# Two graph layers on 64 graphs, one core: the last two graphs' leaky ReLU, output and softmax sums on other engines, and new orders for the first and last four graphs

## The chip, the cores and the metric

The kernel runs on one core of a Trainium2 chip. TensorE (PE in the profile, PEld for its weight loads), VectorE (DVE), ScalarE (ACT), GpSimd (POOL) and SyncE (SP, which issues the DMAs) each work through their own queue in order and wait on semaphores for one another. The metric is the device time of one execution in microseconds.

## The reference

There are 64 graphs of 256 nodes with 256 features, and an adjacency of zeros and ones. Everything is float32. Each graph passes two layers, cut here to what matters:

```python
# layer 0: attention (8 heads of 32), values chosen by edge type, then a feed-forward of 1024
attn = softmax(q @ k.T / sqrt(32))
out = sum((attn * (adj == r)) @ v[r] for r in range(4))      # adj is 0 or 1
x = ln(src + out @ Wo); x = ln(x + gelu(x @ W1) @ W2)
# layer 1: attention over the edges only, with a leaky ReLU on the scores
e = q @ k.T; e = where(e >= 0, e, 0.2 * e)
h = softmax(where(adj > 0, e, -9e15)) @ v
y = ln(concat(ln(h), x) @ Wffn.T) * g2 + b2 + x
```

## The kernel before

One graph is a program of about 122 to 142 operations ("op" in the code), each with one engine, the tiles that it reads and writes, and the instructions that it emits. All programs are put into one list by `in_order`. A graph in the middle takes the due times of `STARTS`, moved by 50 per graph (`PERIOD`). The first four graphs take theirs from `FIRST`, the last four from `LAST`: one number for each op of that graph, of which only the order matters. Each engine's queue is that list, cut down to the engine. Graphs overlap: while one is in layer 1, the next one or two are in layer 0. Tiles come from pools with a few buffers each (`TAGS`), so an op may also wait for a buffer: the score tiles "s" have two, the general PSUM tiles "g" four.

An op is named here by graph and by the tile that it writes, with #2 or #3 for the second or third op on it: 63.e10/0#3 is the third on pair 0 of e10 in graph 63. Scores are kept transposed, keys on partitions, in two halves of 128 keys. A head group hg has four heads, in two pairs (tile names end in hg, a slash and the pair).

In layer 1, after q1 and k1 (ACT copies), each head group runs as follows. TensorE makes the scores s1{hg}0 and s1{hg}1 (`score`, L486). DVE adds the mask, `e = s + neg` (`without_edges`, L511). ACT makes `m = relu(4 s)` (L760). POOL adds `e + m` (L764): with the factor 0.2 in the exp that follows, this is the leaky ReLU. ACT takes the exp (L502). POOL adds the two key halves into es (`halves_added`, L555). TensorE multiplies e with v1 into po[:, 0] (L524) and sums es over the partitions, with ones, into po[:, 1] (L529; `weighted`). DVE divides (L538, L541; `divide`) and takes a minimum for the flags (L546). The heads are turned by TensorE in the edge graphs (L413, through DRAM in the others), normalised (statistics L453 to L457, rs on POOL L462), multiplied with wf (pwa, L365), combined with zb (L784), normalised again (L468), and POOL multiplies by the gain (y2#2, L478) and adds x2 (y2#3, L795) before SP writes the output (L799).

After the last graph DVE checks the flags of all graphs (L807 to L811), TensorE sums over partitions (L813) and DVE writes `bad` (L814). Every engine then loads `bad` and branches past the general path, which isn't needed with these inputs.

The loads of the head are issued by SP in the order of the list: graph 0's x, xT and adj, the weights one by one (`fetch`, L567), and graph 1's.

Of the kernel before, what the change touches and what calls it, by code (L numbers as in the profile page):

```python
# [45 lines left out]
def in_order(programs, starts, period, first, last):  # L46
# [4 lines left out]
    for g, p in enumerate(programs):  # L51
# [75 lines left out]
        -6994.431, -7388.927, -7351.284, -6940.069, -6630.912, -6492.737, -5820.245, -6499.204, -6211.612, -6887.475,  # L127
        -6574.591, -6055.325, -6943.269, -6592.592, -5632.691, -6966.961, -6679.901, -5916.261, -5878.661, -5841.069,
        -7096.532, -7512.778, -6608.876, -6221.265, -5453.387, -5549.194, -6903.347, -6536.598, -6869.405, -6714.282,
        -6284.532, -5847.047, -6310.727, -6096.209, -6434.914, -6237.614, -6127.158, -6105.417, -5766.143, -6278.346,  # L130
        -6188.116, -6047.072, -5658.535, -5527.11, -5365.693, -5365.113, -5411.001, -6000.275, -5717.717, -5900.816,
        -5831.595, -5599.592, -5869.516, -5660.321, -5366.528, -5646.017, -5207.025, -5020.63, -4993.703, -4567.281,
        -4816.977, -4750.625, -4591.773, -4460.957, -4413.934, -4100.038, -4091.573, -4307.485, -3363.907, -4090.816,
        -4014.886, -3947.886, -3817.945, -3833.07, -3724.476, -4057.127, -4027.222, -2952.664, -2920.602, -2866.671,
        -2847.171, -2739.652, -2737.672, -2691.114, -2690.49, -2653.828, -2574.6, -2574.5, -2571.161, -2538.838,
        -2515.46, -2508.392, -2484.851, -2490.055, -2485.753, -2475.11, -2272.412, -1985.028, -1658.536, -1821.102,
        -1771.211, -2129.859, -2036.177, -2076.279, -2024.103, -1654.946, -1088.24, -2129.857, -2050.296, -1834.238,
        -1668.747, -1615.521, -888.839, -844.65, -844.648, -683.087, -2000.703, -2000.701, -1941.643, -1634.963,
        -1305.159, -1117.717, -1867.441, -1519.838, -1476.409, -1286.636, -1065.545, -947.048, -921.545, -905.763,
        -905.336, -659.96, -595.355, -586.09, -600.581, -562.092, -520.989, -499.765, -423.732, -332.149, -138.121,  # L140
        -71.149,
    ],
    [
        -6349.705, -5836.753, -6081.533, -4963.07, -4074.802, -4413.528, -5758.476, -5490.569, -5746.337, -5168.607,
        -5091.359, -4429.3, -4497.965, -4455.15, -5110.005, -4958.379, -4959.155, -4405.675, -4700.068, -5095.014,
        -4918.509, -4648.701, -4492.326, -3784.815, -3591.688, -3574.676, -3462.153, -4751.298, -4193.609, -4058.489,
        -3830.368, -4078.272, -4312.267, -4230.291, -4098.36, -4165.072, -3469.86, -3405.792, -3346.63, -3256.756,
        -3129.133, -3092.291, -3028.461, -2890.16, -2860.984, -2786.263, -2765.467, -2709.294, -1973.087, -2700.693,
        -2592.979, -2679.762, -2547.379, -2572.287, -2562.658, -2234.13, -2091.658, -1352.855, -1285.594, -1154.839,
        -1080.771, -1050.188, -1025.134, -1025.132, -1013.455, -1012.874, -989.144, -989.142, -966.626, -966.624,  # L150
        -860.071, -906.663, -558.44, -710.078, -678.573, -659.959, -657.563, -356.96, -279.865, -204.83, -153.563,
        -570.142, -497.868, -564.88, -400.824, -310.575, -155.647, -529.609, -492.619, -440.991, -372.152, 81.224,
        207.883, 207.885, 208.698, 207.885, -485.015, -297.546, -326.274, -30.803, -30.801, 140.805, -207.171,
        -420.509, 88.779, 94.889, 201.19, 208.257, 208.915, 212.631, 209.017, 218.342, 218.376, 220.881, 220.872,
        226.278, 226.28, 226.608, 226.657, 279.353, 279.888, 293.911,
    ],
    [
        -3383.624, -3282.358, -3383.821, -3315.719, -3292.114, -3276.51, -3278.393, -3143.603, -3202.947, -3127.58,
        -2580.644, -2247.869, -2579.025, -2435.009, -2777.309, -2722.09, -2626.561, -2402.135, -2620.893, -2656.961,
        -2631.065, -2219.459, -2622.132, -2116.303, -2108.283, -1937.208, -2022.273, -2592.872, -2572.894, -2577.864,  # L160
        -2373.389, -2294.93, -2442.259, -2482.641, -2247.275, -2242.874, -2220.102, -2131.046, -2130.146, -2134.458,
        -1791.22, -1730.871, -1604.611, -1586.638, -1465.435, -1440.682, -1117.654, -1046.213, -1042.05, -1130.19,
        -786.309, -989.513, -966.393, -1038.083, -990.527, -1025.728, -1009.818, -865.964, -811.776, -127.986,
        -65.354, 9.746, 82.436, 89.841, 104.183, 109.011, 131.966, 147.965, 147.967, 147.969, 147.971, 147.973,
        166.758, 166.76, 167.18, 214.884, 258.715, 170.464, 170.466, 170.298, 171.246, 185.358, 190.852, 208.774,
        208.776, 175.642, 180.624, 178.747, 185.531, 195.315, 196.259, 178.105, 180.761, 186.235, 190.215, 200.258,
        210.901, 213.291, 215.22, 214.541, 183.413, 187.736, 194.296, 194.298, 196.561, 205.853, 191.477, 188.038,
        192.651, 199.259, 201.622, 209.186, 211.426, 212.75, 212.71, 215.222, 217.141, 221.416, 221.418, 221.42,
        222.631, 226.586, 226.588, 226.78, 228.592, 259.663, 263.707, 276.031,
    ],  # L170
    [
        -2288.419, -2839.379, -2739.277, -1968.859, -600.823, -607.784, -1652.07, -1598.871, -1775.226, -1340.483,
        -845.987, -771.771, -1926.65, -1852.23, -1098.531, -1089.236, -1035.595, -756.952, -991.116, -1065.154,
        -1053.377, -1011.765, -1036.687, -665.969, -442.684, -407.499, -587.218, -955.847, -839.539, -897.643,
        -749.904, -754.104, -907.37, -744.663, -705.697, -900.423, -620.356, -512.637, -437.469, -369.161, -212.408,
        -136.219, -135.814, -82.183, 43.882, 43.884, 105.694, 109.209, 109.211, 122.583, 141.537, 109.636, 115.896,
        115.297, 115.299, 121.125, 131.184, 135.232, 138.719, 155.989, 156.166, 156.168, 156.793, 158.167, 158.169,
        158.2, 158.202, 158.204, 158.206, 158.705, 160.743, 161.464, 161.466, 167.116, 167.118, 188.365, 267.421,
        170.267, 170.269, 172.201, 174.994, 184.139, 184.742, 187.278, 190.613, 176.053, 177.919, 180.678, 186.61,
        198.539, 203.122, 181.22, 179.218, 187.65, 194.89, 195.139, 208.854, 209.532, 216.503, 216.892, 182.467,  # L180
        191.782, 194.246, 194.248, 200.109, 200.111, 187.411, 183.217, 189.468, 195.861, 199.092, 204.103, 206.308,
        208.779, 207.223, 217.154, 220.202, 220.204, 221.864, 221.866, 220.516, 227.932, 227.934, 229.045, 229.512,
        268.016, 268.018, 283.364,
# [3 lines left out]
    [  # L187
        35.967, 81.639, 37.446, 49.047, 111.765, 91.145, 51.709, 55.266, 52.784, 54.975, 49.242, 56.246, 68.373,
        68.375, 60.749, 62.145, 62.145, 69.78, 66.297, 62.145, 63.926, 69.208, 72.044, 76.528, 80.658, 85.349, 80.699,
        67.412, 69.718, 67.414, 75.679, 70.411, 67.899, 68.096, 76.822, 67.901, 76.824, 84.472, 86.349, 81.443,  # L190
        88.348, 91.98, 93.479, 93.837, 95.602, 95.604, 109.765, 109.767, 109.769, 107.231, 118.499, 142.785, 142.787,
        114.816, 116.064, 112.782, 112.784, 135.087, 138.221, 146.498, 149.756, 149.758, 150.979, 150.981, 153.239,
        153.409, 153.411, 153.413, 153.762, 153.864, 153.866, 153.925, 158.963, 160.421, 165.526, 395.103, 433.871,
        168.304, 172.714, 190.173, 198.121, 197.391, 345.395, 688.172, 774.537, 221.708, 371.803, 388.14, 529.792,
        826.449, 1141.164, 359.215, 379.438, 514.717, 977.41, 1368.594, 1442.706, 1601.086, 1657.083, 1545.495,
        611.411, 937.028, 908.733, 1268.399, 1347.288, 1466.055, 731.146, 643.428, 858.041, 1138.369, 1233.238,
        1486.774, 1764.047, 1776.421, 1632.601, 1797.616, 1808.269, 2023.607, 2168.276, 2175.4, 1932.643, 2248.895,
        2261.718, 2261.79, 2261.792, 2340.766, 2357.786, 2448.821,
    ],
# [43 lines left out]
def fast_path(nc, tc, a, out, bad):  # L243
# [13 lines left out]
    with ExitStack() as ctx:  # L257
# [48 lines left out]
        def spread(v):  # L306
            return v[:, None, :].to_broadcast([P, NT, D])
# [14 lines left out]
        def program(g):  # L322
# [3 lines left out]
            def T(name):  # L326
                return at_(g, name)
# [794 lines left out]
```

## Time and profile before

| | us |
|---|---|
| runs: median of 3 (lowest to highest) | 2821.83 (2821.42 to 2822.89) |
| the profiled execution's own time | 2821.28 |
| its span, first to last instruction | 2819.5 |
| TensorE busy | 2780.9 |
| VectorE, ScalarE, GpSimd busy | 2062.9, 1942.1, 2010.9 |

The span is cut into stretches below. For each stretch the profile gives the busy time of each engine, the TensorE clock that was granted (1.00 is full speed) and the share of the DMA engines. The timelines give start, duration, engine, line, operation and tiles, the number of instructions merged into a row, and in brackets the engine's idle time before it with what ended it. A float32 matmul shows as two matmul records, so four instructions are x8.

### The profile page before, as it was taken

The numbers are of one execution on the slowest core, as the hardware profiler recorded it, in microseconds if no ns is written. First come the engines' busy times: TensorE is split into PE (matmuls) and PEld (weight loads), VectorE is DVE, ScalarE is ACT, GpSimd is POOL, SyncE is SP. The second block draws the span as 40 slices with busy tenths as digits, with TensorE's granted clock in tenths as the row PEclk, the third lists the DMA queues.
The fourth block names the chain that finished last, engine by engine and source line by source line (L and its number), as shares of the span: only waits on it lengthen the run. The fifth ranks groups of instructions, "written<-read, shape, count | busy, mean of one in ns | idle before, by whom it ended". The sixth has DMA issues, their size and how long they took to land.

```text
span 2819.5 us, 54187 instructions
## 1 busy us (share of the span) xinstructions
PE 2780.9 (99%) x21062; PEld 2087.6 (74%) x21062; DVE 2062.9 (73%) x3845; ACT 1942.1 (69%) x3135; POOL 2010.9 (71%) x1542
## 2 busy tenths in 40 slices
PE   8999999999999999999999999999999999999996
PEld 6777777777777777777777777777777777777774
DVE  5677777777777777777777777777777777777775
ACT  5766767767767667677677676676776776766763
POOL 3668767677676676776776766867767767667676
PEclk9999999999999999999999999999999999999998
DMA  3012222222222222222222222212222222222200
GB/s 131 23 50 65 59 70 61 53 74 59 57 68 61 61 63 53 73 61 53 72 59 59 66 63 61 63 51 76 58 56 72 57 61 65 58 74 53 59 14 13
DMA packets 269749, 169.54 MB, mean 60 GB/s; under 512 B 18608, under 2 KB 268976, under 8 KB 269488
## 3 DMA queue, kind: packets, MB, share of 16 engines
q1 hardware_dynamic: 269488, 166.02, 22.3%
q8 instruction: 168, 2.75, 0.4%
q14 instruction: 93, 0.76, 0.1%
HBM read 102.77 MB, written 63.18 MB: 59 GB/s over the span
## 4 chain that ended last, share of the span: by engine, by line
PE 96%; DVE 2%; POOL 1%; ACT 1%; issue 0%; DMA 0%; SPq 0%; DVEq 0%; POOLq 0%; ACTq 0%
PE pw L730 15%; PE ph L712 15%; PE po L524 12%; PE s L486 10%; PE pk L351 8%; PE pva L664 8%; PE pq L351 8%; PE pv L365 4%; PE pwa L365 4%; PE pwb L365 4%; PE po L529 4%; PE pwo L365 4%; DVE rd L538 1%; POOL e L764 0%; ACT e L502 0%
## 5 line engine op out<-in xcount | busy, mean ns | idle before, releaser
L555 POOL TENSOR_TENSOR es<-e 128x512 f32<-128x512 f32 x512 | 647.2, 1276 | 578.2 <-issue 434.6
L764 POOL TENSOR_TENSOR e<-e,m 128x1024 f32<-128x1024 f32 x256 | 601.7, 2362 | 92.0 <-DVE e L511 90.5
L712 PE MATMUL ph<-y0T,w 128*128 128x256 f32 x2048 | 465.3, 380 | 0.7 <-ACT y0T L432 0.7
L538 DVE RECIPROCAL rd<-po 128x256 f32<-128x256 f32 x256 | 439.8, 1736 | 31.7 <-PE po L529 31.5
L730 PE MATMUL pw<-w,hT 128*128 128x256 f32 x2048 | 452.8, 379 | 0.0
L502 ACT ACTIVATE e<-e 128x1024 f32<-128x1024 f32 x256 | 268.4, 1050 | 262.0 <-POOL e L764 261.9
L712 PEld LDWEIGHTS ph<-y0T,w 128*128 128x128 f32 x2048 | 387.8, 190 | 81.2 <-issue 17.4
L730 PEld LDWEIGHTS pw<-w,hT 128*128 128x128 f32 x2048 | 389.0, 190 | 52.9
L511 DVE TENSOR_TENSOR m<-s,neg 128x1024 f32<-128x1024 f32 x256 | 310.5, 1216 | 103.2 <-ACT e L502 76.7
L502 ACT ACTIVATE e<-s 128x1024 f32<-128x1024 f32 x256 | 261.1, 1022 | 173.0 <-DVE m L511 90.2
L511 DVE TENSOR_TENSOR e<-s,neg 128x1024 f32<-128x1024 f32 x256 | 305.2, 1214 | 13.4 <-PE s L486 11.0
L760 ACT ACTIVATE m<-s 128x1024 f32<-128x1024 f32 x256 | 256.3, 1026 | 66.7 <-PE s L486 33.6
L486 PE MATMUL s<-q,k 32*128 32x256 f32 x4096 | 294.0, 400 | 2.1 <-ACT q L560 0.7
L524 PE MATMUL po<-e,v 128*32 128x256 f32 x4096 | 272.7, 384 | 8.5 <-ACT v L560 7.9
L486 PEld LDWEIGHTS s<-q,k 32*128 32x128 f32 x4096 | 185.6, 184 | 127.9 <-issue 51.8
L502 ACT ACTIVATE m<-m 128x1024 f32<-128x1024 f32 x256 | 265.6, 1070 | 2.2 <-DVE m L511 2.2
L462 POOL TENSOR_TENSOR rs<-ve,neg_half 128x2 f32<-128x2 f32 x256 | 179.8, 702 | 95.7 <-DVE ve L457 91.5
L664 PE MATMUL pva<-wv,xT 128*128 128x512 f32 x512 | 246.5, 604 | 0.0
L502 ACT ACT_TABLE_LOAD x127 | 162.9, 1283 | 87.7 <-PE s L486 86.3
L719 ACT ACTIVATE hT<-ph,cols 128x256 f32<-128x256 f32 x512 | 208.7, 476 | 12.3 <-PE ph L712 10.7
L672 DVE TENSOR_TENSOR v<-pva,rows 128x512 f32<-128x512 f32 x128 | 87.2, 683 | 167.1 <-PE pva L664 167.1
L524 PEld LDWEIGHTS po<-e,v 128*32 128x32 f32 x4096 | 120.3, 110 | 117.9 <-issue 42.5
(96 smaller groups left out, 4645.9 us busy)
## 6 DMA issues: line engine op xcount, KB each, us to landing
x<-x_dram SPq DMA_DIRECT2D x64, 256.0 KB, 3.0
xT<-xT_dram SPq DMA_DIRECT2D x64, 256.0 KB, 3.3
adj<-adjT_dram SPq DMA_DIRECT2D x64, 256.0 KB, 3.8
out_dram<-y SPq DMA_DIRECT2D x64, 256.0 KB, 2.2
y0d<-y0b SPq DMA_DIRECT2D x236, 64.0 KB, 1.8
y0r<-y0d SPq DMA_DIRECT2D x59, 256.0 KB, 2.8
y1d<-y1b SPq DMA_DIRECT2D x236, 64.0 KB, 1.8
y1r<-y1d SPq DMA_DIRECT2D x59, 256.0 KB, 2.8
```

Source lines behind the costliest of these rows:

```text
L351: nc.tensor.matmul(pt[:, o, :], lhsT=w[:, c, o * P : (o + 1) * P], rhs=s[:, c, :], start=(c == 0), stop=(c == KC - 1),)
L365: nc.tensor.matmul(pt[:, t, :], lhsT=T(s)[:, c, t * P : (t + 1) * P], rhs=w, start=(n == 0), stop=(n == len(parts) - 1),)
L486: nc.tensor.matmul(s[j // 2][:, j % 2, c, :], lhsT=kT[r, hg, c * P : (c + 1) * P], rhs=qT[r, hg, :], start=True, stop=True,)
L502: nc.scalar.activation(T(dst)[:, j], s, AF.Exp, scale=scale, **kw)
L511: lambda: nc.vector.tensor_tensor(T(dst)[:, j], T(src), T("neg")[:, None].to_broadcast([P, 2, NT, D]), ALU.add),
L524: nc.tensor.matmul(po[j * DH : (j + 1) * DH, 0, :], lhsT=v(c, j), rhs=T(e)[:, j, c, :], start=(n == 0 and c == 0), stop=(n == len(parts) - ...
L538: op("DVE", [po], [f"{rd}:rd"], lambda: nc.vector.reciprocal(T(rd), T(po)[:, 1, :]))
L555: lambda: on.tensor_tensor(T(dst)[:, j], T(e)[:, j, 0, :], T(e)[:, j, 1, :], ALU.add),
L664: nc.tensor.matmul(pv.rearrange("p r d -> p (r d)"), lhsT=s[:, c, t * P : (t + 1) * P], rhs=wv0[:, c].rearrange("p r d -> p (r d)"), start ...
L712: nc.tensor.matmul(ph[:, i, :], lhsT=w1[:, c, (f + i) * P : (f + i + 1) * P], rhs=s[:, c, :], start=(c == 0), stop=(c == KC - 1),)
L730: nc.tensor.matmul(T("pw2")[:, t, :], lhsT=T("hT")[:, f + i, t * P : (t + 1) * P], rhs=w2[:, f + i, :], start=(f + i == 0), stop=(f + i == ...
L764: nc.gpsimd.tensor_tensor(T(f"e1{hg}")[:, j], T(f"e1{hg}")[:, j], T(f"m1{hg}")[:, j], ALU.add)
```

## The change

It has two parts. First, in graphs 62 and 63 (`alone`):

- Pair 0 of each head group has its leaky ReLU as one `scalar_tensor_tensor` on DVE, `max(0.2 e, e)`, in place, with both inputs in SBUF; its exp has factor 1. Pair 1 stays as before: Relu on ACT, addition on POOL.
- es is not made in layer 1: TensorE sums both key halves of e itself, in two accumulating passes with ones.
- The gain and the addition of x2 at the output are on DVE.

Second, `FIRST` and `LAST` have new numbers for all eight edge graphs. `STARTS` and `PERIOD` stay.

```diff
+            alone = g >= B - 2
...
-            def rows_op(dst, src, other, alu, also=()):
+            def rows_op(dst, src, other, alu, also=(), eng="POOL"):
...
-                op("POOL", [src, *also], [dst], lambda: nc.gpsimd.tensor_tensor(T(name), T(src), spread(other), alu))
+                on = nc.vector if eng == "DVE" else nc.gpsimd
+                op(eng, [src, *also], [dst], lambda: on.tensor_tensor(T(name), T(src), spread(other), alu))
...
-                    for j in range(HPG):
-                        nc.tensor.matmul(
-                            po[j * DH : (j + 1) * DH, 1, :], lhsT=ones[:, :DH], rhs=T(sums)[:, j, :],
-                            start=True, stop=True,
-                        )
+                    chunks = [T(e)[:, :, c, :] for c in range(NT)] if sums is None else [T(sums)]
+                    for c, es in enumerate(chunks):
+                        for j in range(HPG):
+                            nc.tensor.matmul(
+                                po[j * DH : (j + 1) * DH, 1, :], lhsT=ones[:, :DH], rhs=es[:, j, :],
+                                start=(c == 0), stop=(c == len(chunks) - 1),
+                            )
...
+                    def emit_leaky_dve(hg=hg, pair=pair):
+                        e = T(f"e1{hg}")[:, 2 * pair : 2 * pair + 2]
+                        nc.vector.scalar_tensor_tensor(e, e, ALPHA, e, ALU.mult, ALU.max)
+
+                    if alone and pair == 0:
+                        op("DVE", [f"e1{hg}/{pair}"], [f"e1{hg}/{pair}"], emit_leaky_dve)
+                        exps(f"e1{hg}", f"e1{hg}", 1.0, pair, 4 + 2 * hg + pair)
+                        continue
...
-                    halves_added("POOL", f"e1{hg}", f"es1{hg}", pair)
+                    if not alone:
+                        halves_added("POOL", f"e1{hg}", f"es1{hg}", pair)
...
-                    "PE", ["v1", *(f"{t}1{hg}/{p}" for t in ("e", "es") for p in range(2))], [f"po1{hg}:g"],
+                    "PE", ["v1", *(f"{t}1{hg}/{p}" for t in ("e", "es")[: 1 if alone else 2] for p in range(2))],
...
-            rows_op("y2", "y2", g21, ALU.mult, ["c_rows1"])
+            rows_op("y2", "y2", g21, ALU.mult, ["c_rows1"], "DVE" if alone else "POOL")
+            eng = nc.vector if alone else nc.gpsimd
...
-                "POOL", ["y2", "x2"], ["y2"],
-                lambda: nc.gpsimd.tensor_tensor(T("y2"), T("y2"), T("x2"), ALU.add),
+                "DVE" if alone else "POOL", ["y2", "x2"], ["y2"],
+                lambda: eng.tensor_tensor(T("y2"), T("y2"), T("x2"), ALU.add),
```

What the new numbers do to the queues at the two ends (DVE:po10 is the minimum for the flags; pw2#9 the addition to pw2; pwa#2 the combination with zb):

```
SP before: 0.x wk0 cols 0.xT wq0 wfT wv01 wk1 rows0 0.adj wq1 rows1 wo 1.xT w2 wv1 1.adj w1 1.x
SP after:  0.xT cols wk0 wq0 0.x wfT wv01 rows0 0.adj wk1 wq1 wo 1.xT w2 rows1 w1 1.x wv1 1.adj
PE before: 0.pq0 0.pk0 0.pbf 0.s000 0.pva1 0.pva0 0.s010 0.pmean 1.pq0 1.pk0 0.po00 0.po01 1.s000
PE after:  0.pk0 0.pq0 0.pbf 0.s000 0.pva1 0.pva0 0.s010 0.pmean 1.pk0 1.pq0 0.po00 0.po01 1.s000
DVE before: 0.wide 0.c_wv 0.m00/1 0.m00/0 0.v0/1 0.c_scaled 0.m01/0 0.v0/0 0.c_wf 0.m01/1
DVE after:  0.wide 0.c_wv 0.m00/1 0.m00/0 0.c_scaled 0.m01/0 0.v0/1 0.v0/0 0.m01/1 0.c_wf

PE before, from the end of 62.pw2: 63.py0 61.po11 61.po10 62.py1 63.ph0 62.pk1 61.po1 61.pwa 62.pq1
  63.ph2 62.s100 63.ph6 62.pv1 62.s110 63.ph4 63.pw2..pw2#3 62.pwb 63.pw2#4..#8 62.po11 62.po10 63.py1
  62.po1 62.pwa 63.pk1 63.pq1 63.s100 63.pwb 63.s110 63.pv1 63.po10 63.po11 63.po1 63.pwa
PE after:  63.py0 61.po11 61.po10 62.py1 63.ph0 62.pk1 61.po1 61.pwa 62.pq1
  62.pv1 62.s100 63.ph6 63.ph2 62.s110 63.ph4 62.pwb 63.pw2..pw2#5 62.po10 63.pw2#6..#8 62.po11 62.po1
  63.py1 62.pwa 63.pk1 63.pq1 63.s100 63.pwb 63.s110 63.pv1 63.po10 63.po11 63.po1 63.pwa
DVE after, graph 63: 62.y2 62.y2#2 62.y2#3 63.e10/0 63.e10/1 63.e10/0#2 63.zb 63.e11/0 63.e11/1 63.e11/0#2
  63.rd10 63.DVE:po10 63.o1/0 63.rd11 63.o1/1 63.DVE:po11 63.mv2 63.pwa#2 63.mv3 63.y2 63.y2#2 63.y2#3
ACT after, graph 63: 63.k1 63.q1 63.m10/1 63.m11/1 63.e10/1#3 63.e10/0#3 63.v1 63.e11/0#3 63.e11/1#3
POOL after, end: 62.e10/1#2 62.e11/1#2 63.rs1 63.x2 62.rs2 63.x2#2 62.rs3 63.e10/1#2 63.e11/1#2 63.rs2 63.rs3
```

## The prediction

> **What bounds the kernel now.** I read the page's busy times first, then the windows, which say where TensorE rests, then the timelines of both ends.
>
> ```profile
> PE 2780.9 (99%) x21062; PEld 2087.6 (74%) x21062; DVE 2062.9 (73%) x3845; ACT 1942.1 (69%) x3135; POOL 2010.9 (71%) x1542
> ...
> 0.00:20.00 20.00, 11.85 (x60) 7.77 (x60) 5.38 (x13) 6.04 (x11) 3.77 (x9) 1.00 0.91 296
> 20.00:40.00 20.00, 18.77 (x159) 11.77 (x157) 17.94 (x30) 14.25 (x25) 10.10 (x10) 1.00 0.41 139
> 40.00:2590.00 2550.00, 2550.00 (x19401) 1917.43 (x19403) 1888.35 (x3510) 1792.06 (x2892) 1836.08 (x1406) 1.00 0.23 60
> 2590.00:2740.00 150.00, 148.42 (x1122) 112.16 (x1117) 108.71 (x208) 101.91 (x166) 112.88 (x86) 1.00 0.16 43
> 2740.00:2780.00 40.00, 36.35 (x220) 28.68 (x218) 24.55 (x57) 18.62 (x31) 27.22 (x21) 0.96 0.02 8
> 2780.00:2800.00 20.00, 11.04 (x96) 6.51 (x96) 7.92 (x9) 9.21 (x14) 16.73 (x10) 0.83 0.04 14
> 2800.00:2819.50 19.50, 4.43 (x14) 3.25 (x14) 10.08 (x26) 0.00 (x0) 4.08 (x4) 0.66 0.05 16
> ```
>
> Columns: stretch, length, busy time of PE, PEld, DVE, ACT and POOL, granted clock, DMA share and rate. From 40 to 2590 us TensorE never rests; nothing can be won there. It rests 9.4 us in the first 40, 1.6 before 2740, and 27.7 in the last 80.
>
> ```profile
> 2781.67 2.36 DVE L511 TENSOR_TENSOR e<-s,neg 128x1024 f32<-128x1024 f32 x2 [1.21 <-PE s L486]
> ...
> 2784.11 9.27 POOL L764 TENSOR_TENSOR e<-e,m 128x1024 f32<-128x1024 f32 x4 [0.94 <-DVE e L511]
> ...
> 2793.41 1.06 ACT L502 ACTIVATE e<-e 128x1024 f32<-128x1024 f32 x1 [1.15 <-POOL e L764]
> ...
> 2795.09 1.94 PE L524 MATMUL po<-e,v 128*32 128x256 f32 x16 [7.95 <-ACT v L560]
> ...
> 2802.19 0.42 DVE L541 TENSOR_TENSOR o<-po,rd 128x256 f32<-128x256 f32 x1
> ...
> 2809.77 1.00 DVE L468 TENSOR_SCALAR y<-pwa,mv,rs 128x256 f32<-128x256 f32 x2 [0.81 <-POOL rs L462]
> 2810.68 0.42 DVE L807 TENSOR_SCALAR flags<-flags 128x512 f32<-128x512 f32 x1
> ...
> 2813.92 0.15 DVE L814 TENSOR_SCALAR bad<-pheld 1x1 int32<-1x1 f32 x1 [0.37 <-PE pheld L813]
> ```
>
> In the last graph four leaky additions stand in line on POOL, each released exp by exp to ACT, and TensorE waits 7.95 us, behind v1, which ACT's queue has after the exps. After the last y, DVE checks the flags; the span ends 5.4 us behind bad.
>
> **The change: the totals.** Over graphs 62 and 63, POOL loses four leaky additions (2.36 each), eight key sums (1.28) and four output operations (1.28): 24.8 us. ACT loses four Relus (1.02). DVE gains four scalar_tensor_tensor of 1024 and four operations of 512. TensorE gains eight matmul records for each of four po: the row x8 of L529 is 0.43 us warm in the chain, so 1.7 us. Only what lies on the end's path counts, so I walk both ends.
>
> The leaky itself has no row. L784, the same operation on 256, takes 0.49; 768 more elements at L511/L443's slope of 0.94 ns (1.18 against 0.70 for 512 more) make 1.2 to 1.3; I take 1.2. An output operation on DVE is like L443: 0.70.
>
> **The head.** Now the first matmul waits for the fifth load:
>
> ```profile
> wk<-L_gnn_Wk_dram SPq DMA_DIRECT2D x1, 256.0 KB, 3.0
> ...
> wq<-L_gnn_Wq_dram SPq DMA_DIRECT2D x1, 256.0 KB, 4.9
> ```
>
> wk is issued at 1.22, wq at 2.71 and lands at 7.6. The new SP order is xT, cols, wk, wq, x, and TensorE begins with pk. wk, third at 1.73, lands at about 4.7: start 4.8, not 7.72. But pbf then needs wfT, sixth in both (issued 3.22, landing 7.2 later, 10.4), and scores queue behind it: s000 at 11.4 against 14.1. Next, adj loses one 256 KB load ahead of it (landing 13.6 for 14.3): neg 14.3, two mask additions to 16.7, s010 there against 18.8; with c_scaled moved ahead, pmean ends near 18.9 for 21.2. 1.xT gains 0.9 MB in the queue and is in time; rows1, moved behind w2, lands near 21.8 by bytes, ahead of its user on DVE (c_shifts, after c_wf); were it later, rd00 and so pwo, queued behind, would be late one for one. w1, wv1 and 1.adj end by 26.5 as the last load does now, and 1.adj's first mask addition is at 29 on DVE. The walk to ph ends 2.4 early. I keep 2.3, and subtract 0.3 where 2.m00/1 now stands ahead of 0.y1 on DVE: **-2.0** (between -2.8 and 0).
>
> **The middle.** The 1.6 us before 2740 are searched too; orders can win 1.2 or lose 0.5. I put 0: the walk shows no release there.
>
> **The tail**, from 62.pw2's end, 2735.46 in both. Graph 62 has slack: its two leakies on DVE (2754.5 and 2760.4, each once behind POOL) are done before the exps ask, or 0.5 late if POOL goes first twice. Its po10, with its doubled sums, is put between blocks of 63.pw2, and po1 ahead of py1. Exps follow the last gelu's table load and end at 2763.8, as against 2764.6; both po cost 1.72 instead of 1.29. TensorE then has pw2 done at 2767.7, po11 at 2769.4; DVE's rd and o end at 2771.7, y1 at 2772.6, pwa (2.6 as now) at 2775.7, 63's pk and pq, q1 at 2780.0, s100 done 2781.15, 0.5 earlier than now. Graph 62's y2 is on DVE ahead of 63's masks: y2 ends 2779.75, two operations of 0.70 to 2781.2: s100's own time covers them, just. Anything later in y2 delays e10/0, and all behind it, one for one.
>
> Graph 63 on DVE: e10/0 2781.25-2782.4, e10/1 to 2783.6, leaky to 2784.8, zb to 2785.5, e11/0 2786.7, e11/1 2787.9, leaky 2789.1. POOL keeps two leakies, not four. Here a rule speaks against the change. This trace has DVE operations with both inputs in SBUF just once beside POOL:
>
> ```profile
> 23.96 1.48 POOL L555 TENSOR_TENSOR es<-e 128x512 f32<-128x512 f32 x1 [0.68 <-ACT e L502]
> ...
> 23.90 0.41 DVE L600 TENSOR_TENSOR rows<-rows 128x256 f32<-128x256 f32 x1
> 24.23 1.50 DVE L601 TENSOR_TENSOR rows<-rows 128x256 f32<-128x256 f32 x1
> ```
>
> The same operation took 0.41 and, with POOL running, 1.50; POOL's took 1.48 for 1.28. The Trainium skill, "SBUF — State Buffer", section "Who interferes with whom", says why: a DVE instruction with two SBUF inputs and a GpSimd one that reads SBUF exclude each other for the whole instruction. Both leakies (DVE's and POOL's) become ready when the second mask addition ends; DVE is nearer (0.03 us gap against 0.07). So POOL starts behind DVE: 2784.8-2787.15 and 2789.1-2791.5. Exps: 2788.25, 2789.3, v1 2789.9, e11/0 2790.95, e11/1 2792.6. Without the exclusion, the last would be 1.2 earlier.
>
> po10 starts at 2789.95 (5.1 earlier). The clock decides its price:
>
> ```profile
> 2790.00:2792.00 2.00, 0.00 (x0) 0.00 (x0) 0.00 (x0) 1.40 (x3) 2.00 (x2) 1.00 0.00 0
> 2792.00:2794.00 2.00, 0.00 (x0) 0.00 (x0) 0.00 (x0) 0.85 (x3) 2.00 (x2) 0.61 0.00 0
> 2794.00:2796.00 2.00, 0.91 (x12) 0.46 (x16) 0.00 (x0) 1.03 (x3) 2.00 (x3) 0.50 0.00 0
> ```
>
> Idle from 2787.1, the clock fell to half only near 2792.8, 5.7 us later, and po ran at half. New idle: 2786.1 to 2789.95, 3.85 us. "TensorE: Matmul & The Clock Gate", "What's actually happening", lets it fall after one idle window of about 3.4 us, with free phase. By that earliest case each po costs 3.4, po11 ends 2796.0 and o1/1 2798.2 (now 2802.62): 4.4 won. By the row it is warm: po11 2792.65-2794.4, rd 1.75, o 0.42: 2796.6, 6.0 won. I take the row, since a full window must fit into 3.85.
>
> From o1/1 to y2 nothing changes (8.15 us). Then y2's two operations stand on DVE ahead of the flags, where they lay beside them on POOL: +1.4. The output DMA leaves 1.4 earlier and lands 2.1 later, before the flags' end: no cost. Tail: **-6.0 + 1.4 = -4.6** (-5.8 without exclusion, -3.0 cold).
>
> Sum: -2.0 - 4.6 = -6.6. The profiled execution took 2821.28 (span 2819.5), so 2814.7; the median shown is 0.55 higher, 2821.83, so **2815.2**.
>
> **The rivals.**
> - Cold clock, or POOL wins the shared port at one leaky: each leaky lost costs up to 2.4, the clock 1.6. Tail -3.0 to -1.5: 2816.8 to 2818.3. For it: 3.85 exceeds 3.4. Against: the 5.7 measured. 0.20.
> - The head's gain is lost: the first loads share one stream, so wk and wfT land later or a later wait absorbs it. For: DMA share 0.91 in the first 20 us. Against: xT and wk are moved ahead of x, no bytes are added. Tail alone: 2817.2. 0.15.
> - More: no exclusion (-1.2) and the middle's idle mostly gone (-1.2): 2812.8. 0.12.
> - Slower: the exclusion itself. POOL goes first at all four leakies and DVE reads its two inputs at half rate, 2.6 each. Graph 62's po10 then waits till 2766.7, holding 63.pw2 behind it, +3.3; in 63 e11/1 is ready at 2798.85, po11 cold to 2802.3, o1/1 2804.45: +1.8, flags +1.4, head -2.0: +4.5, 2826.3. It decides once the four leakies run late by about 7 us together. Against: L600's 0.41 is as quick as L541's with PSUM. 0.03.
>
> That the work does not move is excluded: the changed queues have the new operations in the last two graphs and there alone.
>
> **How the numbers follow.** My case has 0.50. A measurement of this kernel can tell about 0.2%, 5.6 us, from no change: the border is 2816.2. My case lies 1 us beyond it, so 0.42 of its 0.50 count as faster, with 0.12 of the larger gain, 0.08 of the first rival and 0.06 of the second: 0.68. Slower by as much: 0.03; the rest, 0.29, within. Range: from 2811.5 (larger gain, plus the head's bound) to 2819.2 (tail at -2.6 and no head).
>
> **What would show it.** First matmul near 4.8 and pmean's end near 19; wait of po for v1 near 4, not 7.95, at granted clock 1.0; leaky on DVE 1.2 to 1.3, or 2 to 3.6 if it lost the port; POOL's leaky stretched to 3.5; L807's successor 1.4 behind y2. Wrong if TensorE rests between 40 and 2590, or if s100 of graph 63 comes later than 2780.4 less the head's gain.

## The result, and the profile after

| | us |
| --- | --- |
| before, median of 11 runs | 2822.57 (2821.02 to 2823.05) |
| after, median of 11 runs | 2815.45 (2812.52 to 2818.98) |
| ratio after to before, 95% interval | 0.9979 (0.9971 to 0.9987) |
| predicted | 2815.2 (2811.5 to 2819.2) |
| profiled execution of after, its span | 2813.84, 2812.1 |

By the ratio the changed kernel is faster by 0.21%, 5.9 us, between 3.7 and 8.2; the two medians differ by 7.1. Its eleven times fall into two groups: six of 2812.52 to 2815.45 us (their median 2813.5) at a mean granted clock of 0.998, and five of 2818.21 to 2818.98 (2818.55) at 0.996. The median of all eleven is the slowest of the lower group. The kernel before spreads over 2 us only, at 0.995 to 0.996 wherever its clock is on record. The profiled execution belongs to the lower group; the clock experiments below say what the two groups are.

The busy line, and the same stretches as before the change:

```profile
PE 2779.5 (99%) x21094; PEld 2085.7 (74%) x21094; DVE 2071.8 (74%) x3853; ACT 1939.3 (69%) x3131; POOL 1988.2 (71%) x1526
...
0.00:20.00 20.00, 14.12 (x65) 9.27 (x66) 7.06 (x14) 6.03 (x10) 5.05 (x10) 1.00 0.90 295
20.00:40.00 20.00, 18.43 (x158) 11.83 (x158) 16.85 (x29) 14.87 (x27) 9.48 (x9) 1.00 0.48 162
40.00:2590.00 2550.00, 2548.71 (x19396) 1915.80 (x19398) 1889.02 (x3511) 1792.77 (x2892) 1836.55 (x1406) 1.00 0.23 60
2590.00:2740.00 150.00, 148.58 (x1127) 112.34 (x1120) 109.25 (x206) 101.93 (x164) 110.85 (x85) 1.00 0.15 40
2740.00:2780.00 40.00, 36.27 (x243) 28.12 (x245) 28.81 (x60) 16.76 (x29) 18.34 (x15) 1.00 0.02 7
2780.00:2800.00 20.00, 13.24 (x124) 8.18 (x116) 15.66 (x24) 6.91 (x11) 7.26 (x3) 1.00 0.05 15
2800.00:2812.10 12.10, 0.19 (x2) 0.11 (x2) 5.19 (x15) 0.00 (x0) 0.69 (x1) 0.57 0.09 26
```

POOL has 22.7 us less work (the walk had 24.8) and DVE 8.9 more. In the first 40 us TensorE rests 7.45 us, not 9.38. But between 40 and 2590, where it had never rested, it now rests 1.3. And the granted clock from 2740 to 2800, which had been 0.96 and then 0.83, is 1.00 in this execution; it falls only behind 2800, where TensorE has almost nothing left to do.

The end of graph 63, from the timeline of all engines:

```profile
2779.69 0.69 DVE L479 TENSOR_TENSOR y<-y,rows 128x512 f32<-128x512 f32 x1
2780.42 0.69 DVE L811 TENSOR_TENSOR y<-y,x 128x512 f32<-128x512 f32 x1
...
2781.03 2.35 DVE L512 TENSOR_TENSOR e<-s,neg 128x1024 f32<-128x1024 f32 x2
...
2783.29 1.21 DVE L772 SCALAR_TENSOR_TENSOR e<-e 128x1024 f32<-128x1024 f32 x1
...
2783.45 3.28 POOL L768 TENSOR_TENSOR e<-e,m 128x1024 f32<-128x1024 f32 x1 [4.83 <-DVE e L512]
...
2788.86 0.56 ACT L564 COPY v<-pv 128x512 f32<-128x512 f32 x1
...
2789.47 1.07 PE L526 MATMUL po<-e,v 128*32 128x256 f32 x16 [2.99 <-ACT v L564]
...
2795.72 0.42 DVE L545 TENSOR_TENSOR o<-po,rd 128x256 f32<-128x256 f32 x1
...
2796.59 1.89 PE L365 MATMUL pwa<-wf,o 128*128 128x256 f32 x8
...
2801.80 0.99 DVE L468 TENSOR_SCALAR y<-pwa,mv,rs 128x256 f32<-128x256 f32 x2 [0.81 <-POOL rs L462]
...
2804.49 0.21 DVE L824 TENSOR_SCALAR flags<-flags 128x64 f32<-128x64 f32 x1
...
2806.33 0.15 DVE L830 TENSOR_SCALAR bad<-pheld 1x1 int32<-1x1 f32 x1 [0.37 <-PE pheld L829]
```

The lines of graph 62's output operations and the masks show how close the cover is: the mask addition starts as they end, about 0.3 us after its scores were done. Then DVE's leaky takes 1.21 and POOL's, which becomes ready at the same moment, 3.28 for 2.36. TensorE waits 2.99 us for v1, not 7.95, and each po runs at full clock (1.07 for 1.94). Two more rows of the kernel before are needed for comparison, 63.pwa and the second operation on the flags:

```profile
2803.36 3.25 PE L365 MATMUL pwa<-wf,o 128*128 128x256 f32 x8
...
2811.02 1.28 DVE L808 TENSOR_SCALAR flags<-flags 128x64 f32<-128x64 f32 x1
```

They took 3.25 and 1.28 us there; the same operations take 1.89 and 0.21 here.

The head, from TensorE's timeline:

```profile
5.24 3.75 PE L351 MATMUL pk<-xT,wk 128*128 128x256 f32 x8 [5.24 <-DMA wk<-L_gnn_Wk_dram]
...
12.35 1.15 PE L487 MATMUL s<-q,k 32*128 32x256 f32 x16
...
18.86 1.13 PE L624 MATMUL pmean<-wf,mean_w 128*128 128x256 f32 x4 [0.45 <-DVE wf L620]
...
37.86 7.20 PE L716 MATMUL ph<-y0T,w 128*128 128x256 f32 x32 [0.87 <-ACT y0T L432]
...
162.36 1.15 PE L487 MATMUL s<-q,k 32*128 32x256 f32 x16 [0.64 <-ACT q L564]
...
209.69 1.24 PE L487 MATMUL s<-q,k 32*128 32x256 f32 x16 [0.53 <-ACT k L564]
...
2728.18 7.07 PE L734 MATMUL pw<-w,hT 128*128 128x256 f32 x32
```

In the kernel before, the rows of ph and of 62.pw2 are

```profile
39.01 6.34 PE L712 MATMUL ph<-y0T,w 128*128 128x256 f32 x28 [0.65 <-ACT y0T L432]
...
2728.37 7.07 PE L730 MATMUL pw<-w,hT 128*128 128x256 f32 x32
```

The first matmul is 2.48 us earlier than before and ph 1.15. Two waits that the kernel before does not have (0.64 and 0.53 us; between 150 and 250 its TensorE is busy for 100.00 of 100 us, here for 98.83) take the 1.15 back: 62.pw2 is 0.2 us earlier, and that is what is left of the head where the tail begins.

So the profiled execution won 0.2 us ahead of the tail and 7.2 in it (from the end of 62.pw2 to the span's end 84.06 us before, 76.85 after). The prediction had 2.0 and 4.6. These are two single executions: that of old_first, below, has the old head too, and its ph starts at 40.62, 1.6 us later than in the kernel before. What the head is worth is for the runs to say.

### The profile page after: what moved, and what is told of

The parts are those of the page before. It is cut to its first block, busy times and chain, and to the rows that moved or that the text cites. A ratio compares the mean times of both kernels' runs of the same rounds, so it can differ in the third digit from the quotient of the medians.

```text
span 2812.1 us, 54239 instructions
## 1 busy us (share of the span) xinstructions
PE 2779.5 (99%) x21094; PEld 2085.7 (74%) x21094; DVE 2071.8 (74%) x3853; ACT 1939.3 (69%) x3131; POOL 1988.2 (71%) x1526
## 4 chain that ended last, share of the span: by engine, by line
PE 93%; DVE 3%; POOL 1%; ACT 1%; DMA 1%; issue 1%; SPq 0%; DVEq 0%; POOLq 0%; ACTq 0%
PE pw L734 15%; PE ph L716 15%; PE po L526 12%; PE s L487 9%; PE pk L351 8%; PE pva L668 8%; PE pq L351 7%; PE pv L365 4%; PE pwo L365 4%; PE po L533 4%; PE pwb L365 4%; PE pwa L365 4%; DVE rd L542 1%; POOL e L768 1%; DVE e L512 0%
## 5 line engine op out<-in xcount | busy, mean ns | idle before, releaser
L559 POOL TENSOR_TENSOR es<-e 128x512 f32<-128x512 f32 x504 | 636.8, 1275 | 582.9 <-issue 455.8
L768 POOL TENSOR_TENSOR e<-e,m 128x1024 f32<-128x1024 f32 x252 | 595.2, 2374 | 103.1 <-DVE e L512 95.1
```

The lines of the kernel that those rows point to most:

```text
L559: lambda: on.tensor_tensor(T(dst)[:, j], T(e)[:, j, 0, :], T(e)[:, j, 1, :], ALU.add),
L768: nc.gpsimd.tensor_tensor(T(f"e1{hg}")[:, j], T(f"e1{hg}")[:, j], T(f"m1{hg}")[:, j], ALU.add)
```

## Experiments: the head

**old_first**: the changed kernel with the old numbers of `FIRST`.

```diff
-FIRST = (new numbers)
+FIRST = (numbers of the kernel before)
```

> The changed kernel with FIRST of before (the first four graphs in their old orders); LAST and the moved operations stay. My account after the result: the new head gains 1.2 us up to the first ph and gives it back in two waits between 100 and 250 us, so the head's share of the gain is about 0.2 us: this kernel should take the time of the changed kernel within 1 us, with 62.pw2 ending at about 2735.5. Theory of the prediction (the head is worth 2.0): 2 us slower than the changed kernel.

Measured: 2814.89 us (2814.43 to 2818.26, nine runs), ratio to before 0.9977 (0.9967 to 0.9987): the same as with the new ones. Its times are in two groups as well, and in the lower ones the new orders are ahead by 1.1 us (2813.5 for 2814.6), in the medians of all runs behind by 0.6. The head's orders add nothing that can be told from zero.

**new_first**: the kernel before with the new `FIRST` alone.

```diff
-FIRST = (old numbers)
+FIRST = (numbers of the changed kernel)
```

> The kernel before with FIRST of the changed kernel only. My account: first matmul at 5.2, ph at 37.9, and 62.pw2 at about 2735.3, so 0.2 us faster than before at most. Theory of the prediction: 2.0 us faster.

Measured: 2821.32 us (2820.40 to 2822.03, thirteen runs), ratio 0.9999 (0.9991 to 1.0008). Alone it is worth nothing either. Its profile has the same two waits (0.64 us at 163.83, 0.40 at 211.03), and in that execution the clock also fell to 0.50 at ph, between 38 and 40 us, so that the step behind ph started 1.6 us later than in the changed kernel's (46.62 for 44.98, from the same start of ph). In both, the new order leaves TensorE resting twice ahead of ph (0.58 and 0.87 us), and only in one did the clock fall.

**loads_first**: is the early start worthless, or does this order lose it? The kernel before, with its own orders but for the first ten loads and the two first matmul groups.

```diff
 # SP, graph 0
-x wk0 cols xT wq0 wfT wv01 wk1 rows0 adj
+xT cols wk0 wq0 x wfT wv01 rows0 adj wk1
 # PE, graph 0
-pq0 pk0
+pk0 pq0
```

> The kernel before with one piece of the new head: SP's order begins xT, cols, wk, wq, x, wfT, wv01, rows0, adj, wk1, and pk0 stands ahead of pq0 on TensorE; all else as before. If the head's gain is given back because the new orders of graphs 0 to 3 wait at 162 and 209 us, this one keeps it: first matmul at 5.2, everything later about 1.2 us earlier, and no rest of TensorE between 40 and 2590: 1.2 us faster than before. If any head start is given back later whatever the order (a wait that does not move with the start), within 0.3 us of before.

Measured: 2818.45 us (2817.53 to 2820.51, 21 runs), ratio 0.9989 (0.9983 to 0.9996), or 3.2 us: more than I had expected. TensorE's timeline:

```profile
36.52 7.20 PE L722 MATMUL ph<-y0T,w 128*128 128x256 f32 x32 [0.66 <-ACT y0T L442]
...
2725.41 7.07 PE L740 MATMUL pw<-w,hT 128*128 128x256 f32 x32
```

ph is 2.5 us earlier than in the kernel before and 62.pw2 3.0 us: no rest in the middle takes it back. The early loads were worth what the walk gave them; it is the other numbers of the new `FIRST` that lose it, first ahead of pmean, then at 162 and 209. Against this trace the changed kernel's is later by 0.72 us at the first scores (12.35 for 11.63), 1.11 at pmean (18.86 for 17.75) and 1.34 at ph. Two causes can be seen. In the new order ACT copies q ahead of k, though TensorE makes pk first (q at 11.09 and k at 11.82; here k at 9.15 and q at 10.87). And c_scaled, moved ahead on DVE, fell beside POOL's key sums and took 1.59 us for 0.61; pmean waited 0.45 for it.

## Experiments: the tail

**moves_only**: the changed code (leaky and output on DVE, sums on TensorE) in the old orders of both ends.

```diff
-FIRST, LAST = (new numbers)
+FIRST, LAST = (old numbers, op by op)
```

> The moved operations of graphs 62 and 63 with FIRST and LAST of before: each remaining operation keeps its old place, the leaky on VectorE the place of POOL's, the output operations theirs. If the tail's gain is the moves' (POOL has two leaky additions in line, not four): 4 us or more faster than before. If it needs the new order (v1 ahead of the last exps on ACT, the output of graph 62 ahead of the masks, po10 between the blocks of pw2): within 2 us of before.

Measured: 2822.94 us (2819.94 to 2824.37, thirteen runs), ratio 1.0003 (0.9995 to 1.0011): the moves alone win nothing. ACT's and TensorE's timelines show where it stays:

```profile
2792.85 1.06 ACT L512 ACTIVATE e<-e 128x1024 f32<-128x1024 f32 x1 [1.00 <-POOL e L777]
...
2794.52 1.93 PE L535 MATMUL po<-e,v 128*32 128x256 f32 x16 [7.04 <-ACT v L573]
```

In the old order v1 is behind ACT's last exp. The last leaky addition ends only 0.6 us earlier than in the kernel before (2792.81 for 2793.38), since in the first head group POOL went first and held DVE's leaky (2.32 us), and the second group's masks stand behind it on DVE. The copy that TensorE waits for still stands behind the exp of that last one, and the doubled sums come on top, at half clock.

**moves_v1**: moves_only with one number changed, that of 63.v1, which now comes ahead of the two exps of the second head group.

```diff
 # ACT, graph 63, end
-exps of e10, exps of e11, v1
+exps of e10, v1, exps of e11
```

> The moved operations with the old orders and one change of order: on ACT, graph 63's copy of v1 stands ahead of the exps of e11 in place of behind them. In the moves alone po10 started at 2794.5 behind v1, at half clock. My theory: the moves free the exps early, but in ACT's queue v1 stands behind the last of them, so TensorE gets nothing; with v1 ahead po10 starts near 2790 and po11 waits only for its own exps: 2.5 us (cold) to 4.5 us (warm) faster than the moves alone, so 2818.5 to 2820.5. If other parts of the new order carry the gain: within 1 us of the moves alone.

Measured: 2817.39 us (2816.36 to 2818.78, 21 runs), ratio to before 0.9985 (0.9979 to 0.9992). Between the medians that is 5.5 us from one copy's place; with each kernel set against the runs of the kernel before beside it (2822.09 and 2821.50), it is 5.0, somewhat more than I had expected.

```profile
2790.83 1.07 PE L535 MATMUL po<-e,v 128*32 128x256 f32 x16 [2.46 <-ACT v L573]
...
2799.58 2.93 PE L374 MATMUL pwa<-wf,o 128*128 128x256 f32 x8
```

Two things come at once: po is not held (2.46 us of waiting for 7.04), and in this execution it runs at full clock. That the shorter rest is why is not shown: behind a rest of 2.06 us, a few rows on, pwa takes 2.93 us for 1.89.

**v1_late**: the opposite, the changed kernel with 63.v1 behind the last exp.

```diff
 # ACT, graph 63, end
-e10/1#3 e10/0#3 v1 e11/0#3 e11/1#3
+e10/1#3 e10/0#3 e11/0#3 e11/1#3 v1
```

> The changed kernel with graph 63's v1 put back behind the last exp on ACT. By the trace po10 would start near 2792.5 in place of 2789.5: 2.0 us later at full clock, and up to 5.4 where the rest of 6 us lets the clock fall. If v1's place is not what counts: within 0.5 us.

Measured: 2819.61 us (2816.49 to 2822.72, thirteen runs), ratio 0.9993 (0.9984 to 1.0001): between medians 4.2 us slower than the changed kernel, and no longer to be told from the kernel before. The profiled execution, of 2821.40 us, has po at half clock again:

```profile
2795.45 1.93 PE L535 MATMUL po<-e,v 128*32 128x256 f32 x16 [5.93 <-ACT v L573]
```

Put in a row, each step changing one thing and each taken against the kernel before beside it: the moves alone +0.9 us, with v1's new place -4.1, with the rest of the new `LAST` (this is old_first) -6.8, with the new `FIRST` -7.1. The other orders of the tail are thus worth some 2.7 us. The kernel before with v1's new place and no moves was not run, so whether the place alone would have won something is open.

**sums_pool**: the changed kernel with the key sums of the last two graphs back on POOL, behind the second leaky.

```diff
-if not alone:
-    halves_added("POOL", f"e1{hg}", f"es1{hg}", pair)
+halves_added("POOL", f"e1{hg}", f"es1{hg}", pair)
...
-None if alone else f"es1{hg}", f"po1{hg}",
+f"es1{hg}", f"po1{hg}",
```

> The changed kernel with the key sums of graphs 62 and 63 back on POOL (eight operations of 1.28 us, behind the second leaky addition), TensorE summing one half. In graph 63 POOL then ends two sums of e11 after the last exp, one or two of them on the path: po's ones must wait, and TensorE's second pass of 0.43 us falls away twice. I expect 1.5 to 3 us slower than the changed kernel at the same clock; if the sums are hidden, within 0.5 us.

Measured: 2820.07 us (2818.21 to 2823.04, 21 runs), ratio 0.9995 (0.9988 to 1.0001). Between medians the sums on TensorE are worth 4.6 us. But all 21 runs have a mean granted clock of 0.995 to 0.996, as the changed kernel's upper group; against that group's 2818.55 it is 1.5 us, at the low end of what I had expected at the same clock. The rest is that with the sums on POOL no run was warm; why is not shown.

```profile
2763.95 0.63 PE L542 MATMUL po<-es,ones 128*32 128x256 f32 x4 [0.28 <-POOL es L568]
2765.17 0.62 PE L542 MATMUL po<-es,ones 128*32 128x256 f32 x4 [0.60 <-POOL es L568]
...
2792.72 4.94 POOL L568 TENSOR_TENSOR es<-e 128x512 f32<-128x512 f32 x4
...
2794.05 1.07 PE L542 MATMUL po<-es,ones 128*32 128x256 f32 x4 [0.67 <-POOL es L568]
```

In each graph TensorE waits for POOL's sums between pieces of po, and in this execution its clock is down at both ends of the tail. These three waits come to 1.55 us; 1.7 us of extra matmuls spare TensorE the queue of 4.94 us on POOL.

**y2_pool**: the changed kernel with the output's gain and addition back on POOL.

```diff
-rows_op("y2", "y2", g21, ALU.mult, ["c_rows1"], "DVE" if alone else "POOL")
+rows_op("y2", "y2", g21, ALU.mult, ["c_rows1"])
...
-"DVE" if alone else "POOL", ["y2", "x2"], ["y2"],
+"POOL", ["y2", "x2"], ["y2"],
```

> The changed kernel with the output's two operations of graphs 62 and 63 back on POOL. The prediction's term: on VectorE they cost 1.4 us at the end, ahead of the flags, so undoing them makes it 1.4 us faster. My account after the result: one flags operation took 1.28 us beside POOL's output operation and 0.21 alone, so undoing gives 3.15 us from the last y to bad in place of 3.53: 0.4 us faster at the end, and within 1 us in all.

Measured: 2815.29 us (2813.10 to 2818.93, twelve runs), ratio 0.9978 (0.9970 to 0.9987): no difference. The timeline says why the 1.4 us that I charged are not there:

```profile
2803.69 1.38 POOL L479 TENSOR_TENSOR y<-y,rows 128x512 f32<-128x512 f32 x1 [1.11 <-DVE y L468]
2803.86 1.28 DVE L824 TENSOR_SCALAR flags<-flags 128x64 f32<-128x64 f32 x1
```

Here, as in the kernel before (L808), this operation on the flags takes 1.28 us beside POOL's; in the changed kernel, without POOL beside it, 0.21. From the end of y2's normalisation to bad it is 3.15 us with POOL and 3.54 with DVE: by the traces the move costs 0.4, less than these runs can tell.

**one_psum**: is it the two SBUF inputs that stretch POOL's leaky? DVE's leaky takes its second input, ahead of the maximum, from the scores in PSUM. This leaves the mask out of that input for pair 0.

```diff
-nc.vector.scalar_tensor_tensor(e, e, ALPHA, e, ALU.mult, ALU.max)
+nc.vector.scalar_tensor_tensor(e, e, ALPHA, T(f"s1{hg}{pair}"), ALU.mult, ALU.max)
```

> The changed kernel with VectorE's leaky of pair 0 reading its second input from the score tile in PSUM in place of e in SBUF; this leaves the mask out of pair 0 of the last two graphs. Same operation, sizes and places, but one SBUF input. If two SBUF inputs exclude POOL: its additions beside it take 2.36 us in place of 3.28 to 3.36, and the blocked leaky of graph 62 takes 1.2 in place of 2.36. If the stretch has another cause, 3.3 stays.

Measured once, 2818.24 us:

```profile
2759.30 2.36 POOL L768 TENSOR_TENSOR e<-e,m 128x1024 f32<-128x1024 f32 x1 [2.38 <-DVE e L512]
...
2760.38 1.22 DVE L772 SCALAR_TENSOR_TENSOR e<-e,s 128x1024 f32<-128x1024 f32 x1
...
2786.27 1.21 DVE L772 SCALAR_TENSOR_TENSOR e<-e,s 128x1024 f32<-128x1024 f32 x1
...
2786.44 2.36 POOL L768 TENSOR_TENSOR e<-e,m 128x1024 f32<-128x1024 f32 x1 [5.14 <-DVE e L512]
```

The two overlap in time and neither is stretched, whichever goes first. In the changed kernel one of the two always is: POOL 3.36 beside DVE 1.22 at 2752.9 and POOL 3.28 twice in graph 63, where DVE goes first, and DVE once, where POOL does:

```profile
2757.51 2.36 POOL L768 TENSOR_TENSOR e<-e,m 128x1024 f32<-128x1024 f32 x1 [1.26 <-DVE e L512]
...
2758.60 2.36 DVE L772 SCALAR_TENSOR_TENSOR e<-e 128x1024 f32<-128x1024 f32 x1
```

With the same sizes, places and engines, only the second SBUF input is gone: that it makes the two exclude each other is shown. The time does not profit: the leaky now holds the score tile longer, and the masks of the second head group start 3.3 us later than in the changed kernel (2788.32 for 2785.03), where those of the first start 3.0 later. This execution also had cold clock at 62.pwa (3.06 us).

## Experiments: the clock

**busy**: are the two groups of times TensorE's clock? The changed kernel, with matmuls into a tile that is overwritten afterwards put into its rests of the last two graphs.

```diff
+def busy(to, times):
+    for _ in range(times):
+        nc.tensor.matmul(to[:, 0, :], lhsT=ident, rhs=w2[:, 0, :], start=True, stop=True)
...
+if alone and dst == "po1":
+    busy(pt, 4)
...
+if g == B - 1 and dst == "po10":
+    busy(po, 6)
```

> The changed kernel with matmuls whose result is overwritten (4 instructions ahead of po1 of graphs 62 and 63, 6 ahead of po10 of graph 63, about 0.43 us each at full clock) in the places where TensorE rests 2.1, 3.0 and 2.2 us. The changed kernel has two levels of time: 2812.5 to 2815.5 at a mean clock of 0.998, and 2818.2 to 2819.0 at 0.996. If the upper level is the clock that falls in these rests, the upper level goes: all executions between 2812 and 2816 at 0.998. If the levels have another cause (loads, queues), both stay, or the time grows by the added matmuls, up to 6 us at half clock.

Measured: 2813.13 us (2812.41 to 2816.21, seven runs), ratio 0.9970 (0.9959 to 0.9982). None of the runs is near 2818 any more, so the clock in these rests makes the upper group; five runs lie between 2812.4 and 2813.2. The other two are at 2815.8 and 2816.2; the latter was profiled, and its clock fell at the head instead, where nothing had been filled in (ph 8.86 us for 7.20):

```profile
38.00:40.00 2.00, 1.54 (x5) 1.20 (x6) 0.82 (x2) 2.00 (x5) 0.34 (x1) 0.73 0.34 108
40.00:42.00 2.00, 2.00 (x6) 1.62 (x5) 1.13 (x1) 2.00 (x2) 2.00 (x2) 0.50 0.49 159
```

No execution of the changed kernel's upper group was profiled. That of old_first, which has the same tail, shows what such an execution does there. It took 2818.26 us, and its windows (the same columns) and its row of po are

```profile
2774.00:2776.00 2.00, 1.64 (x9) 1.32 (x8) 2.00 (x10) 0.35 (x1) 1.27 (x1) 0.73 0.00 0
2776.00:2778.00 2.00, 2.00 (x6) 1.55 (x6) 0.33 (x1) 0.67 (x2) 1.92 (x2) 0.50 0.03 8
...
2790.00:2792.00 2.00, 0.00 (x0) 0.00 (x0) 1.71 (x2) 2.00 (x4) 1.34 (x1) 0.99 0.00 0
2792.00:2794.00 2.00, 1.32 (x16) 0.63 (x20) 0.00 (x0) 1.72 (x6) 1.93 (x1) 0.50 0.00 0
2794.00:2796.00 2.00, 2.00 (x32) 1.02 (x28) 0.00 (x0) 1.11 (x2) 0.00 (x0) 0.65 0.00 0
...
2792.68 1.93 PE L535 MATMUL po<-e,v 128*32 128x256 f32 x16 [2.99 <-ACT v L573]
```

with 62.pwa at 3.37 us for 1.89, and 63.po10's two halves at 1.93 and 1.54 for 1.07 and 1.05: 2.8 us in these three rows. Its wait for v1 was 2.99 us, to the hundredth that of the profiled changed kernel, which stayed at full clock. By the rows the clock fell at about 2792, 2.3 us into the rest.

The tail's 2.8 us are not all of the 5.0 between the groups. A cold ph costs another 1.6 to 1.7 (new_first, busy), and with it the sum is 4.5. That both fall in the same executions would fit the mean clock of 0.996, where each alone has 0.997 (old_first, busy), but no profile shows it.

**before_busy**: the same for the kernel before, with 3 such matmuls ahead of 63.py1, 3 ahead of 62.po1, 14 ahead of 63.po10 and 4 ahead of 63.po1.

```diff
+FILL = {(63, "py1"): 3, (62, "po1"): 3, (63, "po10"): 14, (63, "po1"): 4}
...
+busy(pt, FILL.get((g, dst), 0))
...
+busy(po, FILL.get((g, dst), 0))
```

> The kernel before with overwritten matmuls in TensorE's rests of the last two graphs (3 instructions ahead of 63.py1, 3 ahead of 62.po1, 14 ahead of 63.po10, 4 ahead of 63.po1, 0.43 us each). If half clock costs what its rows say (pwa 2.63 for 1.73, both po 4.8 for 2.6, the last pwa 3.05 with about 1.0 of it on the path): 4 us faster than before, and so more than half of the changed kernel's gain is the clock. If the waits alone count: within 1 us of before.

Measured: 2817.88 us (2816.25 to 2819.76, 21 runs), ratio 0.9988 (0.9981 to 0.9994). Filling the rests of the kernel before wins 3.6 us, about half of the 7.1 between the medians of the change, with no work moved: so much of its time was cold clock. Its po runs at full clock now (the wait is shorter because the added matmuls stand in it):

```profile
2793.00 1.07 PE L532 MATMUL po<-e,v 128*32 128x256 f32 x16 [1.95 <-ACT v L568]
```

## Experiments: a better version

**best**: the changed kernel's code and `LAST`, the old `FIRST` with the loads and first matmuls of loads_first, and the filled rests of busy.

```diff
-FIRST = (new numbers)
+FIRST = (numbers of loads_first)
...
+if alone and dst == "po1":
+    busy(pt, 4)
...
+if g == B - 1 and dst == "po10":
+    busy(po, 6)
```

> The changed kernel with two edits: FIRST is that of before with the first loads reordered and pk ahead of pq (3.2 us faster than before alone), and TensorE is kept busy ahead of po1 and po10 as before (2813.1). If both gains add: 2810 to 2811, some 12 us faster than before. If the head's gain depends on the rest of the orders: 2813.

Measured: 2811.62 us (2811.03 to 2812.23, five runs), ratio to before 0.9964 (0.9951 to 0.9978). It is 9.9 us below the 2821.50 measured for the kernel before beside it, and 3.8 below the changed kernel's median; its runs form one group. It is 1.5 us below busy, not the 3.2 that the new loads won over the kernel before: the two gains did not quite add, and where the rest went is open.

```profile
2786.88 1.07 PE L543 MATMUL po<-e,v 128*32 128x256 f32 x16 [0.41 <-ACT v L581]
```

## Why the prediction was right or wrong

The time came out by luck: two errors went against each other, and the median of eleven runs happens to be the slowest of the six warm ones. The mechanism in the tail was right.

- **The head, wrong in size: -2.0 predicted, -0.2 in the two profiled executions, nothing that the runs can tell.** The walk had the first matmul at 4.8 (5.24) and the first scores at 11.4 (12.35), pmean ended about 1 later than predicted, in part behind c_scaled, for which the walk charged nothing beside POOL, and ph was 1.15 earlier, not 2.3. The step that failed is "The middle ... I put 0: the walk shows no release there": a walk of the first 40 us ends where new waits begin, and two of them, at 162 and 209 us, took the rest. The rival "a later wait absorbs it" had this; loads_first shows that it isn't a law of the early start, but a property of these orders. The prediction's own sign of being wrong, a rest of TensorE between 40 and 2590, came true here.
- **The tail, right in its mechanism, -4.6 predicted and -7.2 in the profiled execution.** The wait for v1 went from 7.95 to 2.99 (some 4 predicted), po10 began at 2789.47 (2789.95), o1/1 ended at 2796.14 (2796.6). DVE's leaky took 1.21 to 1.22 (1.2 taken), and went first in graph 63, as assumed from the gaps of 0.03 and 0.07 us. That the moves win only with v1's new place is shown by moves_only, moves_v1 and v1_late; sums_pool gives the sums' place 1.5 us at the same clock.
- **The exclusion: confirmed, and priced nearly right.** It makes POOL's leaky 0.9 us longer, where 1.2 was charged. The L600 and L601 rows of before pointed to it, and what the Trainium skill, "SBUF — State Buffer", section "Who interferes with whom", says of two SBUF inputs is what one_psum shows: 3.28 with them, 2.36 without. The slower rival needed POOL to win at all four leakies; it won at one, in graph 62.
- **The flags' +1.4 was mis-sized: +0.4.** I had charged the two operations on DVE, and not seen that L808, 1.28 us beside POOL, would shrink to 0.21.
- **"From o1/1 to y2 nothing changes (8.15)": it became 6.65.** 63.pwa had run at half clock before (3.25 us in the trace), and here took 1.89. I had weighed the clock only for po.
- **The clock: the reason was wrong.** I took the 5.7 us row for the likelier case, "since a full window must fit into 3.85". (The row's 0.61 puts the fall at 2792.4, 5.3 us into the rest. And the cold case was added up wrong: two po of 3.4 from 2789.95 end at 2796.75, not 2796.0.) In old_first the clock fell in a rest of 2.99. "TensorE: Matmul & The Clock Gate", section "What's actually happening", calls the window free-running; the same rest with two outcomes fits its free phase, but not a need for 3.4 us of rest. The rival "cold clock", at 2816.8 to 2818.3 with a chance of 0.20, is near what five of eleven executions do, at 2818.2 to 2819.0; and cold cost not 1.6 but 5.0 us between the groups' medians, for it takes graph 62's pwa too; the three rows of old_first account for 2.8 of it.

In the profiled execution, whose tail was warm: -6.3 to o1/1, -1.5 to y2, +0.4 for the flags, +0.2 behind bad, together -7.2, and -0.2 of head. The range's lower end, 2811.5, is 0.5 below what its own terms give (2812.8 less 0.8). What sets the phase in an execution was not tried and stays open; so do the rest of the gap between the groups and why loads_first won 3.2 us, more than the 2.5 at ph.

## What to carry to other kernels

Relieving an engine moves nothing while the copy that the consumer also needs stands behind the relieved work in another engine's in-order queue: look for the last releaser's place in its queue before moving any work. A short rest of TensorE can cost a second time, in half-clock matmuls behind it, and it does so in some executions only; a few overwritten matmuls in the rests won 2.3 us here (2815.45 to 2813.13), and 3.6 in the kernel before. A gain at the start must be followed to the stage that sets the end before it is counted.

## What had not been expected of the hardware

- Two executions with the same 2.99 us rest of TensorE ahead of po, one at full and one at half clock behind it; between the two groups of times lie 5 us.
- A DVE tensor_scalar of 128x64 with a single SBUF tensor as input took 0.21 us alone and 1.28 beside a POOL operation of 1.38; two of 128x256 (c_scaled) took 0.61 where POOL had just ended (new_first) and 1.59 beside its key sums (the changed kernel). Not only instructions with two SBUF tensors are held up.
